# Cross attention on one Trainium2 core: score matmuls on 32x64 tiles, and running maxima kept with two neighbouring queries side by side

## The chip, the core and the metric

The kernel runs on one core of a Trainium2 chip. Five engines work side by side, each with its own instruction queue: TensorE (PE; its weight loads are shown as PEld), VectorE (DVE), ScalarE (ACT), GpSimd (POOL) and SyncE (SP, which here only issues DMAs). They wait for each other by semaphores. The metric is the device time of one execution in microseconds.

## What is computed

The reference is one layer of three residual blocks on x (4 batches, 128 tokens, 512 channels), all in float32: cross attention to a context of 4 x 2048 tokens, self attention with relative positions, and a gated attention block. The change touches the first block only:

```
q = (layernorm(x) @ Wq + bq)      # 4 x 128 queries, 16 heads of 32 channels
k = (ctx @ Wk + bk);  v = (ctx @ Wv + bv)          # 4 x 2048 keys
scores = einsum('bqhd,bkhd->hbqk', q, k) / sqrt(32)
attn = softmax(scores.reshape(16 * 4, 128, 2048), axis=0)
out = einsum('hbqk,bkhd->bqhd', attn, v)
x = x + out @ Wo + bo
```

The softmax is unusual: it runs over the 64 pairs of head and batch, not over the keys. For each query and each key on its own it therefore needs the maximum and the sum over 64 numbers. Nothing has to be carried from one block of keys to the next except the sum of the outputs.

## The kernel before

**Tiling.** The 2048 keys are worked off in 16 blocks (n) of 128. In one block, the 16 heads are 4 chunks (c) of 4 heads (i); a chunk's 128 channels lie on the 128 partitions, 32 to a head. The scores of one block and one chunk are 4 heads x 4 batches x 128 queries = 2048 numbers for each of the 128 keys; the keys are on the partitions. They come to lie in four PSUM banks, one per head, held as two tiles of 1024 columns (HALF). Within such a half the columns are ordered (f, q): f counts 8 pairs of head and batch, q the 128 queries.

**One block's steps**, each a short word in the lists `first`, `order` and `last` (lines 696 to 726):

- `p`, `q`: the keys' projection, seven block products as in Strassen's scheme (`product`, 326). `y`: the same for the values (`v_product`, 415). Both multiply with `by_columns` (204), which splits a matmul of 128 output rows into four of 32 (4 column groups of the array).
- `sc` (`scores`, 450): the scores of a chunk. For each batch b and head i it multiplies 32 channels (a row group of the array, line 457) by 128 keys and streams 128 queries. Four heads are four row groups.
- `s0`, `s1` (`scores_out`, 467): ScalarE copies each half from PSUM to the SBUF tile `sg`.
- `m0`, `m1` (`largest_of`, 472): VectorE keeps the running maximum `mx` (1024 columns, laid out like a half) over the two halves of the four chunks: one instruction for chunk 0 (L477, from `sg` and the other half in PSUM), two for each later chunk (L479): seven in a block.
- `tl` (`largest_tail`, 488): one reduction over f on VectorE brings `mx` down to 128 numbers in `stat`, which lies in PSUM.
- `sb` (`shifted`): VectorE subtracts them from `sg`. `ex`: ScalarE takes the exponential. `to`, `tt`: GpSimd sums up. `iv`, `ml` (`scaled`): VectorE inverts the sum and multiplies. The lines of `sb` and `ml` are one, L495.
- `wo`, `at`, `eo` (L606, L536, L609): the outputs are summed in PSUM and SBUF, with 4 column groups of 32.

**Order.** The scheduler is switched off (`manual_schedule`, 257): every engine gets its instructions in the order in which the program calls the steps, and the lists spell this order out. In the loop over n (lines 743 to 747) four blocks are in work at once: a word acts on block n, n-1, n-2 or n+1 (the second entry in `steps`). `first` and `last` are the same for the beginning and the end of the pipeline. The next block of the context is loaded by SP two turns ahead.

**Buffers.** The scores have two times two banks (`ps_s`, 253); a chunk's banks are free once `s0`, `s1`, `m0` and `m1` have read them. `mx` has one buffer (`red`, 252).

After the last block, `last` finishes the softmax on TensorE and ends with the projection by Wo; the other two blocks of the layer follow and are not touched. One of their helpers matters for the prediction: `transposed_out` (L974) copies with the same layout of two neighbours side by side (`PAIR` at line 903) into the tile `eT`, and L1052 reads that tile.

Of the kernel before, what the change touches and what calls it, by code (L numbers as in the profile page):

```python
# [9 lines left out]
F32 = mybir.dt.float32  # L10
AF = mybir.ActivationFunctionType
ALU = mybir.AluOpType
AX = mybir.AxisListType
# [3 lines left out]
def perceiver_layer(ctx: ExitStack, tc: tile.TileContext, a: dict, out: bass.AP):  # L17
# [7 lines left out]
    nc = tc.nc  # L25
    P = 128
    B, T, D = a["x"].shape
# [176 lines left out]
    def by_columns(ps, lhsT, rhs, start, stop):  # L204

        for i in range(NH):
# [2 lines left out]
                ps[cols], lhsT=lhsT[:, cols], rhs=rhs, start=start, stop=stop, skip_group_check=True  # L209
            )  # L210

    def project_T(ps, w, src, c):

        for k in range(C):
            nc.tensor.matmul(  # L215
                ps, lhsT=w[:, k, c * P : (c + 1) * P], rhs=src[:, k, :], start=(k == 0), stop=(k == C - 1)
            )
# [26 lines left out]
    def bank(n):  # L244
        return ps_g.tile([P, 512], F32, tag="ps", name=f"ps_{n}")

    with s1:
# [4 lines left out]
        red = s1.enter_context(tc.tile_pool(name="s1_red", bufs=1))  # L252
# [6 lines left out]
        def banks(n):  # L259

            ts = [ps_s.tile([P, 2, 512], F32, tag="pss", name=f"ps4_{n}_{k}") for k in range(2)]
            return [t[:, k, :] for t in ts for k in range(2)], [t.rearrange("p i f -> p (i f)") for t in ts]

        HALF = NH * B * T // 2

        stat = ps_m.tile([P, 4, T], F32, tag="stat", name="stat")
        kT, v, sg, pss, mxs, sms, zs = {}, {}, {}, {}, {}, {}, {}
# [182 lines left out]
        def scores(n, c):  # L450


            ps, pss[n, c] = banks(f"s{n}_{c}")
            for b in range(B):
                cols = slice(b * T, (b + 1) * T)
                for i in range(NH):
                    rows = slice(i * HD, (i + 1) * HD)
                    nc.tensor.matmul(  # L458
                        ps[i][:, cols],
                        lhsT=kT[n, c // 2][rows, c % 2, cols],  # L460
                        rhs=qT[rows, c, cols],
                        start=(b == 0),
                        stop=True,
                        skip_group_check=True,
                    )

        def scores_out(n, c, k):
            if k:
                sg[n, c] = sc.tile([P, NH * B * T], F32, tag="sg", name=f"sg{n}_{c}")
            nc.scalar.copy(sg[n, c][:, k * HALF : (k + 1) * HALF], pss[n, c][k])  # L470

        def largest_of(n, c, k):


            if c == 0 and k == 0:
                mxs[n] = red.tile([P, HALF], F32, tag="mx", name=f"mx{n}")
                nc.vector.tensor_tensor(mxs[n], sg[n, c][:, HALF:], pss[n, c][0], ALU.max)  # L477
            elif c:
                nc.vector.tensor_tensor(mxs[n], mxs[n], pss[n, c][k], ALU.max)  # L479

        def fold_tail(eng, t, out, op):
            w = HALF // 2
            while w > T:
                eng.tensor_tensor(t[:, 0:w], t[:, 0:w], t[:, w : 2 * w], op)
                w //= 2
            eng.tensor_tensor(out, t[:, 0:w], t[:, w : 2 * w], op)

        def largest_tail(n):
            nc.vector.tensor_reduce(  # L489
                stat[:, n % 2, :], mxs[n].rearrange("p (f q) -> p q f", q=T), axis=AX.X, op=ALU.max  # L490
            )

        def over(n, c, row, op):
# [12 lines left out]
        def fold(eng, t, g, first):  # L506
            if first:
                eng.tensor_tensor(t, g[:, 0:HALF], g[:, HALF:], ALU.add)  # L508
            else:
                eng.tensor_tensor(t, t, g[:, 0:HALF], ALU.add)  # L510
                eng.tensor_tensor(t, t, g[:, HALF:], ALU.add)  # L511
# [35 lines left out]
        ps = ps_o.tile([P, B * T], F32, tag="pso", name="warm_ps")[:, 0:P]  # L547
# [5 lines left out]
        ps, _ = banks("k0")  # L553
        for k in range(C):
            for c in range(C):
                nc.tensor.matmul(  # L556
                    ps[c],
                    lhsT=wk[:, k, c * P : (c + 1) * P],
                    rhs=cts[0][:, k, :],
                    start=(k == 0),  # L560
                    stop=(k == C - 1),
# [24 lines left out]
        qT = big.tile([P, C, B * T], F32, tag="qT", name="qT")  # L586
        for c in range(C):
            ps = bank(f"q{c}")
            project_T(ps, wq, xT, c)
            nc.scalar.activation(qT[:, c, :], ps, AF.Identity, bias=bq[:, c : c + 1])  # L590
# [78 lines left out]
        def accumulate(n, c):  # L669
# [9 lines left out]
            "at": (lambda n, c: attend(n, c, pso[n, c], n > 0), -2), "at3": (lambda n: steps["at"][0](n, 3), -3),  # L679
            "eo": (output_out, -2), "eo3": (lambda n: output_out(n, 3), -3),  # L680
            "sc": (scores, 0), "s0": (lambda n, c: scores_out(n, c, 0), 0), "s1": (lambda n, c: scores_out(n, c, 1), 0),
            "m0": (lambda n, c: largest_of(n, c, 0), 0), "m1": (lambda n, c: largest_of(n, c, 1), 0),
            "tl": (largest_tail, -1), "sb": (shifted, -1), "ex": (exponentials_of, -1), "to": (total, -1),
            "tt": (lambda n: total_tail(nc.gpsimd, n), -1), "iv": (inverse, -2), "ml": (scaled, -2),
            "yb": (v_start, 0), "y": (v_product, 0), "ya": (v_copied, 0), "y11": (v_corner_11, 0), "yu": (v_kept, 0),
# [99 lines left out]
    with ExitStack() as s2:  # L785
# [10 lines left out]
        def bank_l(i, n):  # L796
            return psl.tile([P, 512], F32, tag=f"psl{i}", name=f"s2_{n}_{i}")

        qT = one.tile([P, C, B * T], F32, tag="qT", name="qT2")
        kT = one.tile([P, C, B * T], F32, tag="kT", name="kT2")  # L800
# [64 lines left out]
        def queries(c):  # L865
            ps = bank(f"q2_{c}")
            project_T(ps, awq, xT, c)
            nc.scalar.mul(qT[:, c, :], ps, SCALE)

        def keys(c):  # L870
            ps = bank(f"k2_{c}")
            project_T(ps, awk, xT, c)
            nc.scalar.copy(kT[:, c, :], ps)
# [29 lines left out]
        PAIR = 2  # L903
# [139 lines left out]
        def relative_v(part):  # L1043
# [18 lines left out]
        engines = {"v": nc.vector, "g": nc.gpsimd}  # L1062
        steps = {
            "lt": relative_part, "sc": scores, "jn": join, "mx": largest, "ex": exponentials, "iv": inverse,
            "nm": lambda c, i, e: normalised(c, i, engines[e]), "tp": transposed, "cp": transposed_out,
            "av": attend, "oe": attended, "tb": turned_back, "ad": added, "vp": values, "ve": values_out,
# [83 lines left out]
    with ExitStack() as s3:  # L1150
# [35 lines left out]
        q = one.tile([P, B, D], F32, tag="q", name="q3")  # L1186
# [25 lines left out]
        qT = one.tile([P, C, B * T], F32, tag="qT", name="qT3")  # L1212
        kT = one.tile([P, C, B * T], F32, tag="kT", name="kT3")
# [22 lines left out]
        pss = {}  # L1236
# [69 lines left out]
        for b in range(B):  # L1306
            ps = bank_l(f"q{b}")
# [73 lines left out]
        ps = bank("g")[:, 0:P]  # L1381
# [45 lines left out]
        for b in range(B):  # L1427
# [3 lines left out]
            for part in range(parts):  # L1431
                cols = slice(part * D // parts, (part + 1) * D // parts)
                ps = bank_l(f"y{b}_{part}")[:, cols] if b else y0
# [65 lines left out]
```

## Time and profile before

| | |
|---|---|
| median of 3 runs | 777.65 us (777.35 to 778.41) |
| profiled execution: its own time | 776.4 us |
| profiled execution: span of the core | 774.6 us |
| granted TensorE clock, mean | 0.998 |
| PE, DVE, ACT, POOL busy | 97%, 81%, 68%, 59% |
| score matmuls L458 | 2048 records, 76.8 us busy |
| running maxima L477 and L479 | 16 and 96 instructions, 1216 and 1221 ns each |
| reduction L489 | 16 instructions, 2054 ns each |
| subtract and scale L495 | 123 instructions, 2281 ns each |

How to read the profile: a line of the groups view names the source line, the engine, the operation, the tiles (out<-in), the shapes (partitions x elements), the number of instructions, and after the bar the busy time, the mean duration of one, and the engine's idle time just before them with what ended it. For a matmul, "32*128 32x128" is the weight tile (32 rows by 128 columns) and the streamed operand. Busy times of matmuls overlap: a busy PE is not PE at its peak, and the start-to-start time of a group says more than the duration of one record. The chain of waits follows the work back from the last instruction to what released it.

### The profile page before, as it was taken

How to read it: one execution, taken by the hardware profiler on the slowest of the kernel's cores; microseconds unless marked ns; L12 is line 12 of the kernel's file. 1: busy time of each engine (PE TensorE's matmuls, PEld its weight loads, DVE VectorE, ACT ScalarE, POOL GpSimd, SP SyncE). 2: the span in 40 equal slices, each digit the busy share in tenths (PEclk: the TensorE clock that was granted, in tenths of full speed). 3: DMA queues.
4: the chain of work that ended last, by engine and by line, in shares of the span. 5: the costliest groups of instructions: out<-in, count | busy, mean ns of one | idle time of the engine just before them, and what ended most of it. 6: DMA issues, size and time to landing. Idle time of an engine off the chain costs nothing.

```text
span 774.6 us, 28614 instructions
## 1 busy us (share of the span) xinstructions
PE 752.7 (97%) x13027; PEld 470.6 (61%) x13027; DVE 624.8 (81%) x642; ACT 527.6 (68%) x921; POOL 460.3 (59%) x296
## 2 busy tenths in 40 slices
PE   9999999999999999999999999997899999989998
PEld 5446566666666666666666666665253477664574
DVE  2158499999999999999999999998883688856463
ACT  2346777878788787887878878786823247933770
POOL 1713787859577695876958678599870005510261
PEclk9999999999999999999999999999999999999999
DMA  8310101101011010110101001032200005103001
GB/s 303 120 59 3 56 4 57 57 3 58 3 57 58 3 57 3 58 52 8 58 3 57 28 33 57 3 111 64 103 3 1 0 4 219 55 11 104 1 2 54
DMA packets 12619, 38.43 MB, mean 50 GB/s; under 512 B 1249, under 2 KB 1650, under 8 KB 10450
## 3 DMA queue, kind: packets, MB, share of 16 engines
q1 hardware_dynamic: 10802, 33.50, 12.5%
q8 instruction: 102, 1.67, 0.9%
q10 hardware_dynamic: 1248, 2.23, 0.8%
q0 software_dynamic: 448, 0.87, 0.6%
q14 instruction: 19, 0.16, 0.1%
HBM read 34.50 MB, written 2.10 MB: 47 GB/s over the span
## 4 chain that ended last, share of the span: by engine, by line
PE 88%; ACT 5%; DVE 5%; issue 1%; DMA 0%; POOL 0%; DVEq 0%; POOLq 0%; ACTq 0%
PE k L208 20%; PE ps_vu L208 12%; PE ps_s L458 9%; PE ps_vf L208 6%; PE ps_o L536 6%; PE ps_q L215 4%; PE ps_kc L208 3%; PE ps_vc L208 3%; PE ps_v L208 3%; ACT lg L954 2%; PE s_y L1371 2%; PE s_k L215 2%; PE out L208 2%; PE ps_k L215 2%; PE ps_k L556 2%; PE ps_sum L208 2%
## 5 line engine op out<-in xcount | busy, mean ns | idle before, releaser
L495 DVE TENSOR_TENSOR sg<-sg,stat 128x2048 f32<-128x2048 f32 x123 | 277.6, 2281 | 1.3 <-ACT rz L622 0.7
L470 ACT COPY sg<-ps_s 128x1024 f32<-128x1024 f32 x128 | 128.3, 1016 | 36.8 <-PE ps_s L458 22.1
L479 DVE TENSOR_TENSOR mx<-mx,ps_s 128x1024 f32<-128x1024 f32 x96 | 117.2, 1221 | 35.0 <-PE ps_s L458 22.8
L510 POOL TENSOR_TENSOR sm<-sm,sg 128x1024 f32<-128x1024 f32 x45 | 107.5, 2389 | 38.2 <-ACT sg L504 35.9
L504 ACT ACTIVATE sg<-sg 128x2048 f32<-128x2048 f32 x64 | 122.8, 1919 | 4.4 <-DVE sg L495 2.9
L511 POOL TENSOR_TENSOR sm<-sm,sg 128x1024 f32<-128x1024 f32 x45 | 107.5, 2388 | 3.5
L508 POOL TENSOR_TENSOR sm<-sg 128x1024 f32<-128x1024 f32 x16 | 38.3, 2396 | 94.0 <-ACT sg L504 94.0
L208 PE MATMUL k<-s,wk_sums 128*32 128x256 f32 x1440 | 86.7, 381 | 0.0
L458 PE MATMUL ps_s<-qT,kT 32*128 32x128 f32 x2048 | 76.8, 285 | 5.2 <-DVE mx L477 4.0
L458 PEld LDWEIGHTS ps_s<-qT,kT 32*128 32x128 f32 x2048 | 64.3, 188 | 24.6 <-issue 17.0
L208 PEld LDWEIGHTS k<-s,wk_sums 128*32 128x32 f32 x1440 | 43.9, 110 | 29.3 <-POOL s L311 0.2
L536 PE MATMUL ps_o<-sg,v 128*32 128x128 f32 x1792 | 59.6, 274 | 0.1
L536 PEld LDWEIGHTS ps_o<-sg,v 128*32 128x32 f32 x1792 | 51.5, 111 | 10.4 <-issue 1.3
L208 PE MATMUL ps_vu<-wv_sums,s 128*32 128x256 f32 x896 | 53.5, 379 | 0.0
L609 ACT COPY acc<-ps_o 128x512 f32<-128x512 f32 x56 | 32.9, 588 | 25.8 <-PE ps_o L536 24.7
L861 POOL TENSOR_TENSOR lg<-lg,pos 128x512 f32<-128x512 f32 x6 | 7.4, 1283 | 61.5 <-DVE lg L863 61.5
L208 PEld LDWEIGHTS ps_vu<-wv_sums,s 128*32 128x32 f32 x896 | 29.0, 110 | 19.2
L311 POOL TENSOR_TENSOR s<-ct,s 128x512 f32<-128x512 f32 x30 | 39.0, 1300 | 1.3
L311 POOL TENSOR_TENSOR s<-ct 128x512 f32<-128x512 f32 x30 | 38.6, 1287 | 0.2 <-PE ps_vu L208 0.2
L1269 POOL TENSOR_TENSOR e<-e,rs 128x512 f32<-128x512 f32 x16 | 16.3, 1039 | 36.3 <-DVE rs L1268 36.3
L606 ACT COPY ps_o<-acc 128x512 f32<-128x512 f32 x52 | 31.0, 596 | 6.4 <-DVE v L443 5.6
L489 DVE TENSOR_REDUCE stat<-mx 128x128 f32<-128x1024 f32 x16 | 32.9, 2054 | 0.1
(275 smaller groups left out, 1423.6 us busy)
## 6 DMA issues: line engine op xcount, KB each, us to landing
ct<-in_ctxT SPq DMA_DIRECT2D x15, 1024.0 KB, 4.9
ev_win<-in_tabv SPq DMA_DIRECT2D x1, 2048.0 KB
w_xattn_Wk<-in_xattn_Wk ACTq DMA_DIRECT2D x4, 256.0 KB, 6.9
ct<-in_ctxT SPq DMA_DIRECT2D x4, 256.0 KB, 6.7
x<-in_x SPq DMA_DIRECT2D x4, 256.0 KB, 8.5
w_xattn_Wv<-in_xattn_Wv ACTq DMA_DIRECT2D x1, 1024.0 KB, 12.8
w_xattn_Wq<-in_xattn_Wq SPq DMA_DIRECT2D x1, 1024.0 KB, 10.7
x_dram<-x SPq DMA_DIRECT2D x4, 256.0 KB, 2.3
```

Source lines behind the costliest of these rows:

```text
L208: nc.tensor.matmul(ps[cols], lhsT=lhsT[:, cols], rhs=rhs, start=start, stop=stop, skip_group_check=True)
L215: nc.tensor.matmul(ps, lhsT=w[:, k, c * P : (c + 1) * P], rhs=src[:, k, :], start=(k == 0), stop=(k == C - 1))
L311: nc.gpsimd.tensor_tensor(s_, x, y, op)
L458: nc.tensor.matmul(ps[i][:, cols], lhsT=kT[n, c // 2][rows, c % 2, cols], rhs=qT[rows, c, cols], start=(b == 0), stop=True, skip_group_che ...
L470: nc.scalar.copy(sg[n, c][:, k * HALF : (k + 1) * HALF], pss[n, c][k])
L479: nc.vector.tensor_tensor(mxs[n], mxs[n], pss[n, c][k], ALU.max)
L495: nc.vector.tensor_tensor(g, g, stat[:, row, :].unsqueeze(1).to_broadcast([P, NH * B, T]), op)
L504: nc.scalar.activation(sg[n, c], sg[n, c], AF.Exp, scale=SCALE)
L508: eng.tensor_tensor(t, g[:, 0:HALF], g[:, HALF:], ALU.add)
L510: eng.tensor_tensor(t, t, g[:, 0:HALF], ALU.add)
L511: eng.tensor_tensor(t, t, g[:, HALF:], ALU.add)
L536: nc.tensor.matmul(ps[i * HD : (i + 1) * HD, b * T : (b + 1) * T], lhsT=v[n, b // 2][:, b % 2, h * HD : (h + 1) * HD], rhs=sg[n, c][:, f * ...
```

## The change

Two things are changed. First, each score matmul becomes two, for keys 0 to 63 and keys 64 to 127 of the block: the weight tile is 32 x 64 in place of 32 x 128, the output goes to half of the PSUM partitions (a column group of 64), and the same queries are streamed to each. There are twice as many matmuls, in the same order of batches and heads. Second, `mx` is laid out as (64 pairs of queries, 8 f, 2 queries) in place of (8 f, 128 queries). The maxima read the scores in their old order and write `mx` two neighbouring numbers at a time, 64 bytes apart; they read `mx` the same way. The reduction reads, for one query, 8 numbers that are 8 bytes apart where they were 512 bytes apart. The numbers that are computed are the same, and so is the order of the instructions on every engine.

```diff
+    def by_halves(ps, lhsT, rhs, start):
+
+        for i in range(2):
+            cols = slice(i * P // 2, (i + 1) * P // 2)
+            nc.tensor.matmul(ps[cols], lhsT=lhsT[:, cols], rhs=rhs, start=start, stop=True, skip_group_check=True)
+
...
         HALF = NH * B * T // 2
+        PAIR = 2
...
                 for i in range(NH):
                     rows = slice(i * HD, (i + 1) * HD)
-                    nc.tensor.matmul(
-                        ps[i][:, cols],
-                        lhsT=kT[n, c // 2][rows, c % 2, cols],
-                        rhs=qT[rows, c, cols],
-                        start=(b == 0),
-                        stop=True,
-                        skip_group_check=True,
-                    )
+                    by_halves(ps[i][:, cols], kT[n, c // 2][rows, c % 2, cols], qT[rows, c, cols], b == 0)
...
+            def paired(t):
+                return t.rearrange("p (f q r) -> p f q r", q=T // PAIR, r=PAIR)
+
             if c == 0 and k == 0:
-                mxs[n] = red.tile([P, HALF], F32, tag="mx", name=f"mx{n}")
-                nc.vector.tensor_tensor(mxs[n], sg[n, c][:, HALF:], pss[n, c][0], ALU.max)
+                mxs[n] = red.tile([P, T // PAIR, HALF // T, PAIR], F32, tag="mx", name=f"mx{n}")
+            mx = mxs[n].rearrange("p q f r -> p f q r")
+            if c == 0 and k == 0:
+                nc.vector.tensor_tensor(mx, paired(sg[n, c][:, HALF:]), paired(pss[n, c][0]), ALU.max)
             elif c:
-                nc.vector.tensor_tensor(mxs[n], mxs[n], pss[n, c][k], ALU.max)
+                nc.vector.tensor_tensor(mx, mx, paired(pss[n, c][k]), ALU.max)
...
             nc.vector.tensor_reduce(
-                stat[:, n % 2, :], mxs[n].rearrange("p (f q) -> p q f", q=T), axis=AX.X, op=ALU.max
+                stat[:, n % 2, :].rearrange("p (q r) -> p q r", r=PAIR),
+                mxs[n].rearrange("p q f r -> p q r f"),
+                axis=AX.X,
+                op=ALU.max,
             )
```

## The prediction

> **What bounds the kernel now.** I read the page first, engine totals and costliest groups:
>
> ```profile
> PE 752.7 (97%) x13027; PEld 470.6 (61%) x13027; DVE 624.8 (81%) x642; ACT 527.6 (68%) x921; POOL 460.3 (59%) x296
> ...
> L479 DVE TENSOR_TENSOR mx<-mx,ps_s 128x1024 f32<-128x1024 f32 x96 | 117.2, 1221 | 35.0 <-PE ps_s L458 22.8
> ...
> L458 PE MATMUL ps_s<-qT,kT 32*128 32x128 f32 x2048 | 76.8, 285 | 5.2 <-DVE mx L477 4.0
> L458 PEld LDWEIGHTS ps_s<-qT,kT 32*128 32x128 f32 x2048 | 64.3, 188 | 24.6 <-issue 17.0
> ...
> L489 DVE TENSOR_REDUCE stat<-mx 128x128 f32<-128x1024 f32 x16 | 32.9, 2054 | 0.1
> ```
>
> An average says little about one stage, so next one turn of the main loop, from the start of one largest_tail reduction (L489) to the next, as busy time of each engine:
>
> ```profile
> 291.78:324.41 32.63, 32.63 (x712) 21.70 (x706) 31.38 (x22) 26.94 (x36) 24.20 (x15) 1.00 0.11 35
> ```
>
> Columns: stretch, length, PE, PEld, DVE, ACT, POOL, clock, DMA. PE is busy for all of the 32.63 us at full granted clock; DVE for 31.38 us. So TensorE sets the turn, and VectorE is only 1.25 us behind. The waits of PE between 60 and 620 us (in total, times, longest) come to about 11 us, none inside the steady turns:
>
> ```profile
> PE ps_s L458 <- DVE mx L477: 4.0, 1, 4.0
> PE ps_sum L208 <- ACT sg L504: 2.0, 1, 2.0
> ...
> PE k L208 <- DVE kT L366: 0.4, 1, 0.4
> ```
>
> The last reduction (549.4 us) lies on the chain that ended last, and the 2.0 us wait hangs on it:
>
> ```profile
> 549.42 2.10 DVE stat L489
> 551.52 0.02 issue
> 551.55 2.30 DVE sg L495
> 553.85 0.02 issue
> 553.87 1.92 ACT sg L504
> 555.79 0.04 issue
> 555.84 12.27 PE ps_sum L208 x112
> ```
>
> **Part 1: scores in 32x64 tiles.** There are 64 score batches (16 blocks x 4 chunks). One batch is 16 matmuls in the code and 32 records (2048/64): each float32 matmul is run as two records. The timeline of one:
>
> ```profile
> 302.84 1.06 PE L536 MATMUL ps_o<-sg,v 128*32 128x128 f32 x32
> ...
> 303.83 1.17 PE L458 MATMUL ps_s<-qT,kT 32*128 32x128 f32 x32
> ...
> 304.93 0.64 PE L208 MATMUL k<-ct,w_xattn_Wk 128*32 128x256 f32 x8
> ```
>
> A batch owns 303.83 to 304.93, 1.103 us (median of the 64, start to start of the next group). Read record by record: the four row groups start 6.7 ns apart, so there are 8 rounds of 4. Round 2 starts 213 ns after round 1; rounds 2 to 8 start 111.7 ns apart; the next group starts 200 ns after the last record. 213 + 6 x 111.7 + 20 + 200 = 1103.
>
> Why is round 1 long? Its weight loads take 181 ns and nothing hides them, so its matmul records last 372 instead of 270 ns: 102 ns exposed for 128 columns. The groups with 32-column tiles (L208, L536) show the same thing smaller: 403 instead of 379 ns, 24 ns exposed. On the line through both (0.81 ns per column), 64 columns expose about 50 ns.
>
> After the change a batch is 64 records, 8 rounds of 8 tiles (4 row groups x 2 column halves). Each tile still streams 128 queries, so a round cannot be shorter than today's stream: the 32-column tiles with 128 streamed columns (L536) take 109.2 ns a round. New batch: first round 213 - 52 = 161; six rounds at 109.2 to 111.7 = 655 to 670; the last round's eighth tile starts 7 x 6.7 = 47 ns after its first, not 20; exit 200. Sum 1063 to 1078: 25 to 40 ns saved, I take 35. x 64 = **-2.2 us**. The array does the same amount of work in the same number of rounds, hence so little.
>
> Unknown cost: eight concurrent tiles are in no row. From below: if the exit does not follow the later eighth tile, 27 ns more are saved a batch, together -4 us. From above: if the two halves of a row group load one after the other, nothing of the 52 ns is saved and the stagger stays, +27 ns x 64 = +1.7 us; if they also stream one after the other, a batch has 16 rounds of 112 ns, +0.9 us x 64 = +57 us. I take the concurrent case: four column tiles run together in L208 and L536, four row tiles here, and tiles are what is shared in both.
>
> The issue of twice as many records (64 pairs in 0.9 us, 14 ns a pair) is the other doubt. Rows: pairs start 6.7 ns apart within every round; L1052 keeps 18.7 ns a pair for 120 pairs and is then held by its tiles, since its starts are bunched in fours; but after some 250 such pairs it stands 1.38 us on "issue". In the loop a batch of 64 is followed by L536 or L208 groups at 27 or 54 ns a pair, so 128 pairs take 3.8 us or more, and L825 runs 128 pairs in 3.6 us without a stall. I charge nothing. [...]
>
> **Part 2: the reduction.** L489 reads its 8 values per query 512 B apart: 2054 ns for 1024 elements. A reduction over neighbours, 512 elements (L949), takes 672 ns; 512 more elements cost 537 ns (L366 684 ns, L479 1221 ns); so 1024 cost 1209 ns. Now the 8 values lie 8 B apart. No DVE row reads at that distance, so 1209 to 2054; I take 1209 (-0.84 us x 16), nearer in distance to neighbours. Who gets it: in 13 steady turns nobody (DVE is not the bound; its 31.38 becomes 30.5). At 549.4 us the chain does: the 2.0 us wait becomes 1.2, and PE runs on without a gap to 568: **-0.84 us**. The first reduction (63.65 us) leads over two subtractions to the addition L366 for which PE waits 0.39 us: **-0.4 us**, then PE is late itself. The 4.0 us wait at 529 us hangs on PE, ACT copies and L477, not on a reduction: nothing.
>
> **Part 3: the maxima.** Seven tensor_tensor per turn (L477, L479, 1216 to 1221 ns) now write, and six of them read, mx in pairs 64 B apart; the scores are still read straight through. A row for writing pairs: L974 writes eT by pairs, 32 B apart:
>
> ```profile
> L974 DVE COPY eT<-s_t x10: 659/679/691, 658.2 to 676.7; 128x512 f32<-128x512 f32 x10
> ```
>
> Plain 512-element copies on the same engine take 675 to 692 ns, so pairs cost the writer nothing. For reading pairs there is no row: 1221 ns if it is as straight, up to 2.05 us if each element cost what L489's do. I take 1221, the row that it is nearest to. [...]
>
> Other moves: the order on every engine stays, no DMA, no buffer and no wait is added; 2048 more PE instruction pairs are fetched.
>
> **Sum.** -2.2 - 0.84 - 0.4 = -3.4 us against the profiled execution's 776.4 (span 774.6): 773.0. The median of the runs shown is 777.65, 1.25 above it, so I forecast 774.2.
>
> **Rivals.**
> *Halves that load one after the other* (B): +1.7 - 1.2 = +0.5 us, 778.2. For it: all loads of one row group come from the same 32 partitions. Against: L208's four loads share 128 partitions and still run together.
> *Pairs slow the maxima* (C), the slower side: place L479, price (t - 1221 ns) x 7 per turn. It decides once seven of them eat the 1.25 us that VectorE lacks to PE plus the 0.84 us that it gains: 2.09/7 = 0.30 us each, 1.52 us per maximum. At 2.05 us a turn lasts 31.4 - 0.8 + 5.8 = 36.4 us, 3.7 more than now, x 14 (13 turns of the loop and about one more beside it) = +52 us: less the 1.2 at the ends it is 825 to 830. Half way, at 1.64 us, +0.9 x 14: 787.
> *Eight tiles do not run as eight* (D): paced at L1052's 18.7 ns a pair, 8 rounds of 150 ns, a batch of 1.45 us, +0.34 x 64 = +22 us, 798; fully serial +57 us, 834.
> *More than I count* (E): exit without stagger (-4) and more of the waits around 530 and 575 us: 769 to 771.
>
> **How the numbers follow.** Forecast A 0.60 (its own range 771.5 to 776); B 0.15; C 0.11; D 0.10; E 0.04. A and E are faster by over 0.2% (1.55 us, what measurement can tell): 0.64; B is the same: 0.15; C and D slower: 0.21. The range takes A, B, most of E and the lowest ends of C and D: 770.5 to 781.
>
> **What would show it.** Score batches of 1.06 to 1.08 us, first-round matmuls of about 320 ns and steady ones of 270; L489's group at 1.2 us; the maxima still at 1.22; a turn of 32.5 us with PE busy throughout and DVE at 30.5. Wrong would make it: a maximum over 1.5 us, a batch over 1.13 us, or waits of PE on "issue" inside the loop.

## The result

The forecast was 774.2 us, 0.4% faster. Measured: 778.67 us (median of 19 runs, 777.79 to 779.94) after 777.35 us (19 runs, 775.83 to 778.41) before. The ratio is 1.002, with an interval of 1.0014 to 1.0026: the change makes the kernel slower by 1.1 to 2.0 us. The time lies inside the stated range (770.5 to 781), but the forecast said faster and the kernel became slower.

The profiled execution took 779.74 us (span 778.0). The lines of its page that answer to those shown of before:

```profile
PE 757.0 (97%) x15075; PEld 470.8 (61%) x15075; DVE 613.1 (79%) x642; ACT 527.2 (68%) x921; POOL 461.4 (59%) x296
...
L484 DVE TENSOR_TENSOR mx<-mx,ps_s 128x1024 f32<-128x1024 f32 x96 | 117.2, 1221 | 37.7 <-PE ps_s L216 23.4
...
L216 PE MATMUL ps_s<-qT,kT 32*64 32x128 f32 x4096 | 78.5, 280 | 5.2 <-DVE mx L482 4.0
L216 PEld LDWEIGHTS ps_s<-qT,kT 32*64 32x64 f32 x4096 | 62.6, 131 | 24.7 <-issue 17.5
```

VectorE did what was expected: the maxima (now L484) still take 1221 ns, the reduction (now L494) 1220 instead of 2052 ns in the median, and VectorE's busy time fell by 11.7 us.

```profile
L494 DVE TENSOR_REDUCE stat<-mx x16: 1217/1220/1229, 64.9 to 553.8; 128x128 f32<-128x1024 f32 x16
```

The score matmuls (now L216) are busy for 78.5 us after 76.8, where less was expected. Three turns of the main loop as busy time of each engine (stretch, length, PE, PEld, DVE, ACT, POOL, clock, DMA):

```profile
260.55:293.31 32.76, 32.76 (x840) 21.63 (x836) 30.66 (x23) 26.88 (x36) 24.28 (x15) 1.00 0.11 35
293.31:326.92 33.61, 33.16 (x840) 21.92 (x836) 30.65 (x22) 26.89 (x36) 25.17 (x15) 1.00 0.11 35
326.92:359.68 32.76, 32.76 (x840) 21.62 (x836) 30.66 (x22) 26.89 (x36) 23.42 (x15) 1.00 0.11 36
```

A turn is 0.13 us longer than before (32.63), with PE still busy throughout and DVE down to 30.66, as forecast for DVE. One turn in this execution is 0.85 us longer still. In it PE stands still once for 0.45 us, and for no other engine; the profile shows nothing that it waited for ("issue"):

```profile
PE k L208 <- issue: 0.5, 1, 0.5
```

Now one score batch, the timeline of PE:

```profile
280.12 0.81 PE L208 MATMUL ps_vu<-wv_sums,ct 128*32 128x256 f32 x9
280.87 1.21 PE L216 MATMUL ps_s<-qT,kT 32*64 32x128 f32 x64
282.00 0.42 PE L208 MATMUL k<-s,wk_sums 128*32 128x256 f32 x4
```

The median of the 64 batches, start to start of the next group, is 1.136 us, where it was 1.103 and should have become 1.06 to 1.08. The starts of its 64 records, in ns from the first, read one by one from the trace, a round of eight tiles to a line:

```
round 1    0   7  14  20  27  34  40  47
round 2  160 167 174 180 187 194 200 207
round 3  269 276 283 289 296 303 309 316
round 4  379 385 392 399 405 412 419 425
round 5  488 494 501 508 514 529 546 563
round 6  597 620 637 654 670 687 704 706
round 7  720 729 746 763 779 796 813 815
round 8  829 839 855 872 889 905 922 939     next group 1136
```

The first four rounds are the forecast to the nanosecond: second round at 160 (161 expected), then 109 apart, 6.7 ns between tiles. From the middle of the fifth on most tiles start about 16.7 ns apart, the seventh round is 14 ns late (720, not 706), and the last tile starts 110 ns after the first of its round instead of 47. These two make 14 + 63 = 77 ns, and with them the 1063 ns expected at best become 1140; the first round (160, not 161) and the exit (197, not 200) take 4 off: 1136.

**The end of the chain** shows the gain of the reduction:

```profile
553.75 1.24 DVE stat L494
555.02 2.30 DVE sg L503
557.34 1.92 ACT sg L512
559.26 0.04 issue
559.30 12.27 PE ps_sum L208 x112
```

From the last reduction to the end of the span are 224.25 us, 225.2 before.

**The account of the two profiled executions** (span +3.4 us). Their own starts differ by 1.2 us before the first score batch (41.9 and 40.7 us), where nothing is changed. Between the first and the last reduction lie 488.84 us after 485.77, 3.1 us more: 13 turns of +0.13 = +1.7; the long turn +0.85; -0.4 behind the first reduction, as forecast; and the +0.9 that is left goes with the clock. Near 535 us PE stands still for 4 us for the maximum of chunk 0 in both kernels (L477 before, L482 now), and before that wait (3.96 and 4.01 us) ends the granted clock falls from 1.00 to 0.50, from 533.4 us on for 3.4 us in the execution of before and from 535.8 us on for 6.8 us here:

```profile
533.40:536.80 3.40, 3.20 (x52) 2.89 (x56) 3.40 (x4) 2.52 (x3) 2.31 (x2) 0.50 0.00 0
```

```profile
535.90:542.60 6.70, 5.61 (x124) 4.95 (x128) 5.65 (x5) 4.39 (x6) 4.62 (x3) 0.50 0.01 2
```

(The first is before, the second is after; same columns as above.) The length is not fixed by the kernel: in the execution of "One tile after the other" below both lengths occur (3.4 us from 103.1 us on, 6.8 us from 174.8 us on). It goes with some 0.7 of the 1.25 us by which the profiled execution of before lay below its median: of 18 further runs of before three had its mean clock of 0.998 and took 776.45 us in the median, and fifteen had 0.993 to 0.996 and took 777.18. None of the 19 runs of the changed kernel had 0.998; whether the change has a part in that is not shown.

### The profile page after: what moved, and what is told of

Its sections match the earlier page's. It is cut to its first block, busy times and chain, and to the rows that moved or that the text cites. A ratio compares the mean times of both kernels' runs of the same rounds, so it can differ in the third digit from the quotient of the medians.

```text
span 778.0 us, 32706 instructions
## 1 busy us (share of the span) xinstructions
PE 757.0 (97%) x15075; PEld 470.8 (61%) x15075; DVE 613.1 (79%) x642; ACT 527.2 (68%) x921; POOL 461.4 (59%) x296
## 4 chain that ended last, share of the span: by engine, by line
PE 89%; ACT 5%; DVE 4%; issue 1%; DMA 0%; POOL 0%; DVEq 0%; POOLq 0%; ACTq 0%
PE k L208 21%; PE ps_vu L208 12%; PE ps_s L216 9%; PE ps_vf L208 6%; PE ps_o L544 6%; PE ps_q L221 4%; PE ps_kc L208 3%; PE ps_vc L208 3%; PE ps_v L208 3%; ACT lg L962 2%; PE s_y L1379 2%; PE s_k L221 2%; PE out L208 2%; PE ps_k L564 2%; PE ps_k L221 2%; PE ps_sum L208 2%
## 5 line engine op out<-in xcount | busy, mean ns | idle before, releaser
L484 DVE TENSOR_TENSOR mx<-mx,ps_s 128x1024 f32<-128x1024 f32 x96 | 117.2, 1221 | 37.7 <-PE ps_s L216 23.4
L216 PE MATMUL ps_s<-qT,kT 32*64 32x128 f32 x4096 | 78.5, 280 | 5.2 <-DVE mx L482 4.0
L216 PEld LDWEIGHTS ps_s<-qT,kT 32*64 32x64 f32 x4096 | 62.6, 131 | 24.7 <-issue 17.5
L489 POOL TENSOR_TENSOR sm<-sm 128x512 f32<-128x512 f32 (+1 forms) x30 | 30.6, 1022 | 2.4
```

Source lines behind the costliest of these rows:

```text
L216: nc.tensor.matmul(ps[cols], lhsT=lhsT[:, cols], rhs=rhs, start=start, stop=True, skip_group_check=True)
L484: nc.vector.tensor_tensor(mx, mx, paired(pss[n, c][k]), ALU.max)
```

## The experiments

**Theory W.** A batch of 64 record pairs is 128 instructions (each matmul record has its weight load). The theory is an inference from the starts above, where full speed ends after 32 pairs, 64 instructions: TensorE holds about 64 instructions, lets go of them in program order, each when it is complete, and takes in new ones 4.2 ns apart. Before, a batch was exactly 64 instructions, and its second to eighth rounds started 111.7 ns apart to the end. By the theory the second half can now come in only as the first completes. In the starts above, the fourth instruction of the batch (the second record of tile 1) starts at 160, lasts 267 and ends at 427; but for one load at 380, the next weight loads are seen from 459 ns on, the new tiles' 16.7 ns apart. The 4.2 is an estimate: 16.7 ns for the four instructions of one float32 matmul (two records, each with its load). **Rivals** (the letters are those of the experiments, not of the prediction): M, the pairwise maxima cost something; D, the second half is slow for its own reasons (data, place in PSUM, the waits in front of it); A, column halves of one row group get in each other's way in the array; P, only a pace, no window.

### The maxima alone

The changed kernel with the old score matmuls:

```diff
-                    by_halves(ps[i][:, cols], kT[n, c // 2][rows, c % 2, cols], qT[rows, c, cols], b == 0)
+                    nc.tensor.matmul(
+                        ps[i][:, cols],
+                        lhsT=kT[n, c // 2][rows, c % 2, cols],
+                        rhs=qT[rows, c, cols],
+                        start=(b == 0),
+                        stop=True,
+                        skip_group_check=True,
+                    )
```

> The layout of the maxima alone, with the old 32x128 score matmuls. Theory W (what costs time in the changed kernel is that a batch of 64 matmul records, 128 instructions with their weight loads, does not fit a window of about 64 instructions that TensorE holds in flight; the maxima are innocent): score batches stay at 1.103 us, maxima at 1.22 us, reductions at 1.22 us, no pause on instruction supply; 1.2 us faster than before (0.84 at the last reduction, 0.39 at the first), ratio 0.998 to 0.999. Rival M (the pairwise maxima delay something): not faster than before, ratio 1.000 or more.

Measured: 775.65 us (median of 12) beside 777.14 (median of 18) for before in the same series, ratio 0.998 (0.9972 to 0.9989). Its instructions on `mx` (engine, operation, minimum/median/maximum in ns):

```profile
L491 DVE TENSOR_TENSOR mx<-mx,ps_s x96: 1212/1222/1225, 51.3 to 549.9; 128x1024 f32<-128x1024 f32 x96
L489 DVE TENSOR_TENSOR mx<-sg,ps_s x16: 1215/1216/1222, 47.7 to 533.1; 128x1024 f32<-128x1024 f32 x16
L501 DVE TENSOR_REDUCE stat<-mx x16: 1217/1219/1228, 65.0 to 551.1; 128x128 f32<-128x1024 f32 x16
```

The pairs cost the maxima nothing (1222 ns after 1221) and take 0.83 us off each reduction (1219 after 2052 ns). Score batches 1.103 us, a turn 32.63 us, no pause. M falls; this part of the forecast (-1.2 us) stands inside the interval. It is also the version that beats both kernels, if only by 0.2% and 0.4%.

### The halves alone

The reverse: `by_halves` with the old `mx` of before.

> The halved score matmuls alone, with the old layout of the maxima. Theory W: batches of 1.136 us as in the changed kernel, +33 ns x 64 = +2.1 us, and on top of it whatever pauses of instruction supply and stretches of half clock come with it (up to 2 us): ratio 1.003 to 1.005, slower than the whole change by 1.2 us. Rival M (part of the cost is the maxima's): no slower than the whole change, ratio 1.002 or less.

Measured: 779.38 us (median of 6) beside 777.14, ratio 1.003 (1.0019 to 1.0041), +2.2 us. Batches of 1.136 us and turns of 32.76 us, as in the whole change, with the reduction at its old 2.07 us:

```profile
260.55:293.31 32.76, 32.76 (x840) 21.63 (x836) 31.38 (x23) 27.00 (x36) 24.17 (x15) 1.00 0.10 35
```

(One turn is 33.01 us long; it starts at 293.31, as the long turn of the changed kernel does.) The loss is all in the halves: +33 ns x 64 = +2.1 us. The two parts measured apart, -1.5 and +2.2 us, agree with the +1.3 us of the whole within their intervals.

### Halves for the first batch only

If the window of theory W costs the gain, fewer records should keep the shorter first load and avoid the window, unless changing the tile's width costs something itself:

```diff
+                    if b == 0:
+                        by_halves(ps[i][:, cols], kT[n, c // 2][rows, c % 2, cols], qT[rows, c, cols], True)
+                        continue
                     nc.tensor.matmul(
```

> New layout of the maxima; halved score matmuls for the first of the four batches only, 32x128 for the other three: 40 records pairs in place of 64 a score batch, so only the first, exposed weight load is shortened. Theory W without a cost for changing the tile's width inside a batch: rounds at 0, 160, 269 and then 111.7 apart, a batch of 1.05 us, 50 ns x 64 = 3.2 us faster than the run with the maxima alone, ratio 0.994 to 0.995. If changing the width from 64 to 128 columns drains TensorE as the change between row and column tiles does (about 110 ns, and 102 ns of an exposed weight load of 128 columns): a batch of about 1.29 us, +12 us, ratio 1.013 to 1.015.

Measured: 786.87 us, ratio 1.0124 (1.0111 to 1.0137). The batch is two groups of L216 and L468:

```profile
284.38 0.47 PE L216 MATMUL ps_s<-qT,kT 32*64 32x128 f32 x16
284.79 0.95 PE L468 MATMUL ps_s<-qT,kT 32*128 32x128 f32 x24
285.67 0.64 PE L208 MATMUL k<-s,wk_sums 128*32 128x256 f32 x8
```

The first 128-column record starts at 404 ns, 197 after the last 64-column one, and its own round lasts 213 ns again: 1.284 us in all (404 + 880), against 1.29 expected if the change of width costs what the change between row and column tiles does. So a change of the tile's width alone costs as much as the change from row to column groups (200 ns of exit and 213 ns for the next first round in a batch of before). The price here is an exit of 197 to 200 ns after the last record, where in the batch of before the next round follows about 90 ns after the last record of the one ahead (111.7 less 20). "Drains" is the expectation's word for it; the trace shows these times and not what goes on in them.

### Quarters

The other direction, 32x32 tiles, sixteen at a time:

```diff
+                    by_columns(ps[i][:, cols], kT[n, c // 2][rows, c % 2, cols], qT[rows, c, cols], b == 0, True)
```

> Old layout of the maxima; score matmuls on 32x32 tiles, 16 tiles at a time, 128 records a batch with the same 8 rounds of work. Theory W (64 instructions in flight, released in program order when each is complete, so only two of the eight rounds fit): the first two rounds start at 0 and 136 ns, the third not before about 320 and mostly after 550, a batch of 1.8 us, +45 us in all. Rival P (no window, only a pace of 4.2 ns an instruction, 8.4 ns a pair): 128 pairs in 1.07 us, batch about 1.25 us, +10 us. Rival A (tiles of one row group get in each other's way in the array): rounds longer than 109 ns from the second on, evenly.

Measured (one execution): 849.73 us. The batch takes 1.834 us (median); theory W said 1.8, P 1.25. The starts of one batch (at 162.39 us) in ns, tile by tile in the first two rounds, then the following ones:

```
  0   6  13  20  26  33  40  46  53  60  66  73  80  86  93 100
133 140 146 153 160 166 173 180 186 193 200 206 213 220 226 233
318 427 435 452 469 485 502 519 535 552 566 ...
```

Two rounds, 32 pairs, 64 instructions run at full speed, 6 to 7 ns between tiles (in most batches the last two tiles of each round are 8 to 19 ns late); then one record starts at 318, when the first has ended (292), and the rest from 427 on, most of them 16.7 ns apart. Loads and matmuls follow theory W one by one: the 33rd load (instruction 65) starts at 135, after the first load's end at 99; the 33rd matmul (66) at 318 and the 34th load (67) at 322, after the first matmul's end at 292; the 34th matmul (68) at 427, after the end of the fourth instruction at 401. A falls too: 16 tiles run undisturbed through the first 64 instructions, the second round 133 ns after the first. The +72 us are more than the 47 of the batches (64 x 0.731). Some 15 of the other 25 us are PE waiting for nothing that the profile shows (between 60 and 620 us: waited for, total, times, longest; the largest three):

```profile
PE ps_vf L208 <- issue: 4.9, 5, 2.5
PE ps_s L208 <- issue: 4.8, 7, 2.1
PE ps_o L529 <- issue: 4.2, 3, 2.0
```

### A batch cut in two

The halves alone, with the batch of chunk 0 issued as two of 64 instructions, with an attend group between them (`sa` is `scores` for batches 0 and 1, `sd` for 2 and 3):

```diff
-            q.4 tl iv yb wo3 y.1 at3 c21 sc.0 eo3 sb.0 ya sb.1 s1.0 ex.0 q.5 y.2 y.6 c22 y11 q.3
+            q.4 tl iv yb wo3 y.1 sa.0 at3 c21 sd.0 eo3 sb.0 ya sb.1 s1.0 ex.0 q.5 y.2 y.6 c22 y11 q.3
```

> Halved score matmuls, old layout of the maxima; in the main loop the score batch of chunk 0 is cut in two batches of 32 records pairs (batches 0 and 1, then 2 and 3), with the attend group at3 between them; chunks 1 to 3 stay whole. Theory W (64 instructions in flight): each part holds just 64 instructions, so both run without pacing: starts 6.7 ns apart, rounds at 0, 160, 269, 379, next group at 0.626 us; the whole batches of chunks 1 to 3 keep 1.136 us. Rival D (it is the second half itself that is slow, by its data, its keys, its place in PSUM or the waits before it): the second part shows starts 16.7 ns apart. Time: two parts of 0.626 in place of 1.136, some +0.1 us x 13 turns against the halves alone.

Measured (one execution): 781.9 us beside 778.15 for before in the same series, +3.75 us; the halves alone (+2.2) and twelve cut batches (+0.108 each, 2 x 0.622 in place of 1.136) make +3.5. (It is twelve and not 13: `at3` works on block n-3, a fifth block beside the four, and in the first of the 13 turns there is none, so the two parts follow each other.) PE around one cut batch and a whole one before it:

```profile
290.20 1.21 PE L216 MATMUL ps_s<-qT,kT 32*64 32x128 f32 x64
291.33 1.93 PE L208 MATMUL ps_vf<-w_xattn_Wv,s 128*32 128x256 f32 x32
...
296.65 0.69 PE L216 MATMUL ps_s<-qT,kT 32*64 32x128 f32 x32
297.27 1.08 PE L546 MATMUL ps_o<-sg,v 128*32 128x128 f32 x32
298.29 0.69 PE L216 MATMUL ps_s<-qT,kT 32*64 32x128 f32 x32
298.91 1.29 PE L208 MATMUL k<-s,wk_sums 128*32 128x256 f32 x20
```

Both parts take 0.622 us (0.626 expected), with rounds at 0, 160, 269 and 379 and tiles 6.7 ns apart to the end (last start 425). The whole batches of the same execution keep 1.136. The second half is as fast as the first when it comes as a batch of its own: D falls. What makes it slow is that it follows 64 other instructions of the same batch.

### Attend with half the queries

The same doubling of instructions in another tile form, with scores and maxima as before:

```diff
+                    for q in range(2):
                         nc.tensor.matmul(
-                            ps[i * HD : (i + 1) * HD, b * T : (b + 1) * T],
+                            ps[i * HD : (i + 1) * HD, b * T + q * T // 2 : b * T + (q + 1) * T // 2],
...
-                            rhs=sg[n, c][:, f * T : (f + 1) * T],
+                            rhs=sg[n, c][:, f * T + q * T // 2 : f * T + (q + 1) * T // 2],
...
```

> Scores and maxima as before; each attend matmul (128x32 weight tile, 128 queries streamed) is cut into two that stream 64 queries each: 64 records a batch in place of 32, the same work, another tile form, twice the weight loads. Theory W: the first eight rounds run 56 ns apart, then the starts spread to about 16.7 ns within a group and the batch comes to 1.17 us in place of 0.987. Without a window (only twice the fixed cost of a round): 1.08 us. If the cost seen in the changed kernel belonged to the 32x64 tiles of the array, no stretching within this batch either: 1.08 us. +0.18 us x 64 = +12 us, or +6 us.

Measured (one execution): 783.09 us beside 778.15. The batch takes 1.078 us, what was expected without a window: this number of theory W is a miss. Starts are uneven from the beginning on (medians 0, 7, 19, 33, 56, 86, 99, 112) and stay so (335, 340, 353, 366, 391), but rounds keep 56 ns. The expectation had taken the 267 ns to completion of a record with 128 queries; the records with 64 last 219 ns, so by the theory they leave earlier, and with 219 the same reckoning gives about 1.12 us, an estimate made after the run. Between 1.12, 1.08 and 1.078 this run decides little; it does show that 64 pairs in a batch cost no more than the doubled fixed part of a round when four tiles share them and records are short.

### One tile after the other

The halves alone with the loops turned round, so that the same 64 pairs go to the same eight tiles, eight pairs in a row to each:

```diff
+            for i in range(NH):
+                rows = slice(i * HD, (i + 1) * HD)
+                for h in range(2):
+                    keys = slice(h * P // 2, (h + 1) * P // 2)
+                    for b in range(B):
...
```

> Halved score matmuls, old layout of the maxima, with the loops turned round: all four batches of one head and half first, then the next half, the next head. The same 64 record pairs, the same eight tiles, another program order, in which 64 instructions cover four tiles only. Theory W: eight tiles never run together; a batch of about 2.2 us, +1.1 us x 64 = +70 us. Without a window (each tile takes its next matmul when it is free): 1.06 to 1.14 us as in the halves alone.

Measured (one execution): 1069.9 us beside 778.15. PE around one batch:

```profile
300.09 1.06 PE L544 MATMUL ps_o<-sg,v 128*32 128x128 f32 x32
301.07 5.47 PE L466 MATMUL ps_s<-qT,kT 32*64 32x128 f32 x64
306.47 3.64 PE L208 MATMUL k<-ct,w_xattn_Wk 128*32 128x256 f32 x32
```

The median batch is 4.467 us at full clock (this one, longer, ran into a stretch of half clock), four times that of the halves alone. "No window" is out by far, but theory W's 2.2 us is a miss as well. The starts say why: the first tile's records at 0, 160, 269, 378, 487, 596, 705, 815, the second tile's from 493, the third's from 986, the fourth's from 1480. The second tile begins 6 ns after the fifth record of the first (493 after 487), when three of the first still wait. An inference from this one run is a second, smaller limit besides the 64: instructions handed on in program order, and a fourth record waiting for one tile holding up everything behind it. In the changed kernel's order (each tile gets two records in turn) such a limit does not bind in the first four rounds, which run at full speed (6.7 ns between tiles). Nor is it what holds the quarters: the record held back there until 318 is only the third of its tile. (The batches make some 215 of the +292 us; the mean granted clock of this execution was 0.917, and the rest goes with it and was not taken apart.)

## Why the prediction was wrong

- **What bounds the kernel**: right. PE was busy throughout before and after, and each ns of a score batch came back in the turn: 4 x 33 ns = 0.13 us.
- **First round** (213 to 161 ns, halves load side by side): right, 160 ns in every batch but the one with the 4 us wait in it. Rival B named the time best (778.2 us) but by a mechanism that did not happen: the halves of a row group do load together (the first eight loads start within 46 ns and last 128 ns each), and eight tiles stream together (in round 2 eight records of 268 ns start within 47 ns, and round 3 starts 109 ns after it; so the prediction's rival D, eight that do not run as eight, does not hold for rounds 1 to 4; later tiles do start 16.7 ns apart, near D's 18.7, but the rounds still follow each other after 109, 123 and 109 ns, not 150).
- **Steady rounds** at 109 ns: right, but for the seventh, which is 14 ns late.
- **The step that failed** is the paragraph on the issue of twice as many records, "I charge nothing", and with it the stagger of 47 ns in the last round. It looked at the sustained rate of issue (L1052, L825) and at pauses over some 250 pairs, and found both sufficient. What it missed is the number of instructions in one batch: it went from 64 to 128, and full speed ended after the first 64 (6.7 ns between tiles in the first four rounds, some 16.7 ns for most from the middle of the fifth on). Before, every score batch was 32 pairs, and so were the attend batches beside it; none of the rows that I measured the batch by could show what lies beyond. Both signs of being wrong that the prediction named on this point came: a batch over 1.13 us, and a wait of PE on "issue" inside the loop. The term was -35 ns a batch and measured +33, from 1103 to 1136: -53 in the first round, -15 by six rounds at 109.2 instead of 111.7, +14 by the late seventh round, +27 by a last round's stagger of 47 instead of 20 (this was in the forecast), +63 because it was 110 and not 47, and -3 at the exit. 64 x 33 ns = +2.1 us in place of -2.2.
- **The reduction** (1209 ns): right, 1220. The 0.84 us at the last one came, and 0.1 more (225.2 to 224.25 us to the end), and the 0.39 us wait for L366 is gone from the waits. Measured alone 1.5 us, forecast 1.2.
- **The maxima** unchanged at 1221 ns: right; rival C fell. The three numbers for VectorE, each for 1024 elements: pairs 64 B apart 1221 ns, single elements 8 B apart 1220 ns, single elements 512 B apart 2052 ns.
- **How close the starts come**: neighbours go to different tiles and start 6.7 ns apart in the first four rounds, as in the rounds of before: right. That this ends after 32 pairs, with 8 and with 16 tiles, is what I had not weighed.
- **Named as a sign, but not priced**: pauses in the instruction supply inside the loop. One came in the changed kernel's profile (0.85 us) and, with 128 pairs a batch (the quarters), 18 of them, some 15 us in all. The profile lists 118 instruction packets on queue q8 after 102, 16 more for TensorE's 4096 further instructions; away from loads of the context they follow each other after some 3.5 to 7 us, but the one ahead of the pause came only at 318.5, 9.8 us after the one at 308.7. The next context block was being loaded from 314.8 to 318.6, and in all twelve such loads between 118 and 483 us of this execution an instruction packet starts within the last 0.6 us of the load. My inference is that the load holds the packet back in every turn, and that once this took longer than TensorE's supply lasted (8.6 and 9.0 us between packets went without a pause). No run moved the load to test it.

**What stays open.** Shown is that the second half of a batch is slow only behind 64 other instructions (two parts of 64: 0.622 us each, one of 128: 1.136 us), and that full speed ends after 64 with 8 tiles and with 16. That the 64 are let go in program order and on completion is inferred from times (427, 459, and 318, 427 with the quarters), in which the ends of matmul records are the profiler's model, and no run took this apart from other rules with the same times. The attend run does not decide for it, and the rule that a fourth waiting record for a tile blocks rests on one run.

## What to carry to other kernels

Count the instructions of a closely issued group of small matmuls, weight loads included, not only their rate: in these score batches the first 64 ran at the pace of the tiles, and beyond that the pace fell (6.7 to some 16.7 ns between most tiles; 1.136 us where 1.06 was expected for 128 instructions on 8 tiles). Score matmuls split to fill eight tiles ran at the tiles' pace only within that count (0.622 us for a part of 64 instructions, 0.626 expected), and only in an order that gives consecutive matmuls to different tiles (4.467 us a batch in the other order). And look at how far apart in memory a strided reduction reads: a layout with two neighbours side by side cost its writer nothing here (1221 ns before and after) and took 40% off the reader (2052 to 1220 ns).

## What the runs showed of the hardware that was not expected

- The same 64 matmul pairs on the same eight tiles take 1.136 or 4.467 us, by their order in the program alone.
- A change from 64 to 128 weight columns within row groups costs the whole exit (197 ns) and an exposed weight load (213 ns for the round), as a change of the kind of group does (200 and 213 ns in a batch of before).
- In a PE pause of 4 us the granted clock falls to 0.50, for 3.4 us in the profile of before and for 6.8 us in those of the changed kernel and of the first six experiments. By the mean clocks, runs of the same kernel differ in this, and it goes with some 0.7 us, enough to hide half of this change's effect between two single profiles. The length is not all: in the halves alone PE worked for only 3.5 of the 6.8 us (5.6 in the changed kernel), and the last interval between reductions was 28.41 us (29.29 in the changed kernel, 28.24 before).
